# A selective scan: B's diagonals written by ScalarE, one turn of B for both directions, a shift of 64 rows, two states as products

## The chip, the cores and the metric

The kernel runs on one core of a Trainium2 chip. The time is device microseconds of one launch; the kernel before takes 25,224.66 us, the median of 3 runs (25,203.01 to 25,237.02). The profile that is quoted comes from one further execution of 25,254.47 us, with a span of 25,252.7 us from the first to the last instruction.

## What is computed

Four layers run over a batch of 8 images of 192 channels and 64 x 64 pixels in 32-bit floats. Layers 0 and 2 hold a two-dimensional selective scan, and all of the change lies there. For each image, four sequences (rows and columns, each forward and backward) of 4096 positions are scanned with 16 states a channel:

```python
x0 = x.reshape(B, D, L)
x1 = x.transpose(0, 1, 3, 2).reshape(B, D, L)
xs = jnp.stack([x0, x1, x0[..., ::-1], x1[..., ::-1]], axis=1)
x_dbl = jnp.einsum('bkdl,kcd->bkcl', xs, x_proj_weight)
dts, Bs, Cs = jnp.split(x_dbl, [R, R + N], axis=2)
dts = jnp.einsum('bkrl,kdr->bkdl', dts, dt_projs_weight)
A = -jnp.exp(A_logs.astype(jnp.float32)).reshape(K, D, N)
delta = jax.nn.softplus(dts + dt_projs_bias[None, :, :, None])

def step(h, inp):
    u_t, d_t, B_t, C_t = inp
    h = jnp.exp(d_t[..., None] * A) * h + (d_t * u_t)[..., None] * B_t[:, :, None, :]
    y = jnp.einsum('bkdn,bkn->bkd', h, C_t)
    return (h, y)
...
_, ys = jax.lax.scan(step, h0, seq)
```

So for every position, channel and state a decay `exp(dt*A)`, an input `dt*x*B`, a linear recurrence over the positions, and a sum over the 16 states weighted by C. What stands around it (norms, 1x1 and depthwise convolutions, windows and gates) is not touched.

## The kernel before

`scan_layer` is called twice for each of the 8 images, so there are 16 scans. A scan is made of **units** `(d, i, c, v)`: `d` is the direction (0 forward, 1 backward; all forward units come first), `c` one of 8 chunks of `Q = 512` positions, and `v` one of three sets of 128 rows: `v = 0` and `v = 1` are channels 0 to 127 of the one and the other orientation, `v = 2` holds channels 128 to 191 of both (`o` tells the orientations apart, 64 rows each). A scan has 2 x 8 x 3 = 48 units. Three units on one chunk, numbered `m`, are called a **group** here; a scan has 16 groups. A unit is worked in 8 **steps** `j`: each covers one of `NB = 4` blocks of `SB = 128` positions and one half (8) of the `NS = 16` states.

There is no scheduler: the loop over `k` (units) and `j` (steps) at L413 to L473 writes the instructions out by hand, and each engine executes its own in that order (`tc.manual_schedule()`). What a step issues, engine by engine:

- **VectorE**: `scan(k, j)`. For each step a small addition of the carried state to the first column (L306; every second step also a product that makes it, L304) and one hardware scan over 8 states x 128 positions (L309). The additive input is the PSUM tile `u` (two buffers), the factor and the result share the tile `da`.
- **TensorE**: `fill(k, j)` writes `u`. For 4 residues `e` and 2 ways `r` it multiplies a 32-row strip of the turned `dt*x` (`dtt`) with a 32-row strip of a matrix that has B's values on diagonals (`dg`), L288. `add_up` (L345) then sums a block's 16 states by turning each 128 x 128 piece into the PSUM tile `py`; states in `AS_PRODUCT` are multiplied by the identity, the others pass in transpose mode. `project_a/b` (L145, L152, L155) and `steps_a` (L210, L212) make B, C and dt for the group `m + 1`, `turn_a` (L226) turns `dt*x`, `diagonals_a` (L185) turns B, `turn_back` (L363) adds and turns the results of backward units.
- **ScalarE**: `decay(k + 1)` (L245, 16 exponentials of 128 x 512 for the next unit, spread over steps by `DECAY`), `cut(k + 1)` (L254, L255), which saves the first column of the next unit's decays and sets it to zero and which the next unit's first scan needs, `keep` (L316), `take` (L353, the sums out of `py`), `turn_b` (L232, L235), `project_b`'s copies (L159, L160) and `steps_b` (L216, softplus, with two loads of the activation table).
- **GpSimd**: `times_c` (L326, four a unit) and `steps_c` (L220).
- **SyncE** issues all DMAs: the loads of `vs`, C and earlier sums, the stores of C, sums and results.

What the change touches: `xd` holds the projected rows of a group (B in rows 0 to 15, C in 16 to 31, dt's inputs above, for `o = 1` the same from row 64) for 512 positions and a second copy of the first 128 behind them, so that `windows()` can take every fourth position with an offset of `r * SB + e`. The turned B comes out shifted by one block of 32 rows for `r = 1`; `turn_b` makes the matching shifted copy of `dt*x` with four copies of 32 rows (L235), and `fill` picks the strip `q = (s - r) % 4`. `diagonals_b` multiplies a mask (`msk`, 1 where column = row mod 32) with the turned B on VectorE, L195:

```python
            PUT = {(1, 7): (0, 0), (2, 0): (0, 1), (2, 2): (1, 0), (2, 3): (1, 1)}
```

says at which unit and step the four of a group are issued: after the scan of step 7 in the second unit, and of steps 0, 2 and 3 in the third. The PSUM pool `misc` has two buffers that all small TensorE products of a unit take in turn (`project`, `turn_a`, `diagonals_a`, `turn_back`, `steps_a`); a buffer comes free when ScalarE or VectorE has read it.

Of the kernel before, what the change touches and what calls it, by code (L numbers as in the profile page):

```python
# [7 lines left out]
F32 = mybir.dt.float32  # L8
AF = mybir.ActivationFunctionType
ALU = mybir.AluOpType  # L10
# [4 lines left out]
P = 128  # L15
CA, CB = 128, 64
# [4 lines left out]
Q = 512  # L21
NS = 16
SB = 128
# [17 lines left out]
def tile_net(ctx: ExitStack, tc: tile.TileContext, a: dict, out: bass.AP):  # L41
    nc = tc.nc
# [5 lines left out]
    ident = cst.tile([P, P], F32, name="ident")  # L48
# [11 lines left out]
    msk = cst.tile([P, 33], F32, name="msk")  # L60
# [38 lines left out]
    def scan_layer():  # L99
# [5 lines left out]
        with (  # L105
# [15 lines left out]
            nu, nm = len(units), len(units) // 3  # L121
            vt, xd, cdr, dg = {}, {}, {}, {}
            dts, dtx, dtt, das, cts, us = {}, {}, {}, {}, {}, {}
# [6 lines left out]
            def misc():  # L130
                return sp.tile([P, Q], F32, tag="misc", name="misc", bufs=2)
# [17 lines left out]
            def project_b(m):  # L149

                d, px = chunk_of(m)[0], pxs.pop(m)
                nc.tensor.matmul(  # L152
                    px[0:CB], wxt[:, d, 0, 0:CB], vt[m][:, 0, :], start=False, stop=True
                )
                nc.tensor.matmul(  # L155
                    px[CB:P], wxt[:, d, 0, CB:P], vt[m][:, 1, :], start=False, stop=True
                )
                xd[m] = sv.tile([P, Q + SB], F32, tag="xd", name="xd")
                nc.scalar.activation(xd[m][:, 0:Q], px, AF.Identity, bias=msk[:, 32:33])  # L159
                nc.scalar.copy(xd[m][:, Q : Q + SB], xd[m][:, 0:SB])  # L160
                cdr[m] = sd.tile([2, NB, NS, SB], F32, tag="cd", name="cd")
                for o in range(2):
                    nc.sync.dma_start(
                        out=cdr[m][o].rearrange("s n t -> n s t"),
                        in_=xd[m][o * CB + NS : o * CB + 2 * NS, 0:Q].rearrange(
                            "n (s t) -> n s t", t=SB
                        ),
                    )
# [3 lines left out]
            def windows(ways=2):  # L172
                for r in range(ways):
                    for e in range(4):
                        t0 = r * SB + e
                        yield r * 4 + e, slice(t0, t0 + 4 * P - 3, 4)

            bts = {}

            def diagonals_a(m, o):  # L180

                pt = misc()
                rows = slice(o * CB, o * CB + NS)
                for i, cols in windows():
                    nc.tensor.transpose(  # L185
                        pt[:, i * NS : (i + 1) * NS], xd[m][rows, cols], ident[rows, rows]
                    )
                bts[m, o] = pt[:, : 8 * NS].rearrange("p (i n) -> p i n", n=NS)
                dg[m, o] = sw.tile([P, 8, NS // 2, 32], F32, tag=f"dg{o}", name=f"dg{o}")

            def diagonals_b(m, o, r):

                shape = [P, 4, NS // 2, 32]
                at = slice(r * 4, (r + 1) * 4)
                nc.vector.tensor_tensor(  # L195
                    dg[m, o][:, at], msk[:, 0:32].unsqueeze(1).unsqueeze(1).to_broadcast(shape),
                    bts[m, o][:, at, r * 8 : r * 8 + 8].unsqueeze(3).to_broadcast(shape), ALU.mult,
                )


# [27 lines left out]
            def turn_b(k):  # L228

                dtt[k] = sw.tile([P, 2, 4, P], F32, tag="dtt", name="dtt")  # L230
                pt = pts.pop(k).rearrange("p (e c) -> p e c", e=4)
                nc.scalar.copy(dtt[k][:, 0], pt)  # L232
                for q in range(4):
                    r = (q + 1) % 4
                    (nc.scalar.copy if k else nc.vector.tensor_copy)(  # L235
                        dtt[k][q * 32 : (q + 1) * 32, 1], pt[r * 32 : (r + 1) * 32]
                    )

            def decay(k, n0, n1, s=slice(0, NB)):

                d, i, c, v = units[k]
                if n0 == 0 and s.start == 0:
                    das[k] = sw.tile([P, NB, NS, SB], F32, tag="da", name="da", bufs=3)
                for n in range(n0, n1):
                    nc.scalar.activation(  # L245
                        das[k][:, s, n, :], dts[k].rearrange("p (s t) -> p s t", t=SB)[:, s], AF.Exp,
                        scale=neg_a[:, v, d, n : n + 1],
                    )
# [26 lines left out]
            def fill(k, j):  # L275


                d, i, c, v = units[k]
                s = place(k, j)[0]
                u = us[k, j] = sp.tile([P, 8, SB], F32, tag="u", name="u", bufs=2)  # L280
                n = slice(j % 2 * 4, j % 2 * 4 + 4)
                for e in range(4):
                    for r in range(2):
                        q = (s - r) % 4
                        rows = slice(q * 32, (q + 1) * 32)
                        for o in ((v,) if v < 2 else (0, 1)):
                            ch = slice(0, P) if v < 2 else slice(o * CB, (o + 1) * CB)
                            nc.tensor.matmul(  # L288
                                u[ch, r * 4 : r * 4 + 4, e::4], dtt[k][rows, r, e, ch],
                                dg[k // 3, o][rows, r * 4 + e, n], start=True, stop=True,  # L290
                            )

            tmps = {}
# [79 lines left out]
                )  # L373
                nc.sync.dma_start(out=ys[v][:, c * Q : (c + 1) * Q], in_=y)

            AS_PRODUCT = (0, 5, 10)
            DECAY = (
                {0: (0, 4), 1: (4, 7), 2: (7, 11), 4: (11, 14), 5: (14, 16)},
                {0: (0, 4), 1: (4, 8), 4: (8, 12), 5: (12, 16)},
            )  # L380
            PUT = {(1, 7): (0, 0), (2, 0): (0, 1), (2, 2): (1, 0), (2, 3): (1, 1)}

            def has(k):
                return 0 <= k < nu
# [12 lines left out]
            diagonals_a(0, 0)  # L397
            steps_b(2)
            for r in range(2):
                diagonals_b(0, 0, r)  # L400
                load_c(0, r)
            turn_a(0)
            turn_b(0)
            for s in (slice(0, NB // 2), slice(NB // 2, NB)):
                decay(0, 0, NS, s)
                cut(0, s)
                if s.start == 0:
                    steps_c(1)
                    diagonals_a(0, 1)
                    fill(0, 0)  # L410
            for r in range(2):
                diagonals_b(0, 1, r)
            for k in range(nu + 1):  # L413
                m, v = divmod(k, 3)
                ahead = 0 <= m + 1 < nm
                for j in range(8):
# [27 lines left out]
                    if ahead and v == 1 and j == 1:  # L444
# [2 lines left out]
                        steps_a(k + 4)  # L447
                        steps_b(k + 3)
                        steps_b(k + 4)
                    if v > 0 and ahead and j == (6, 1)[v - 1]:  # L450
                        diagonals_a(m + 1, v - 1)
                    if (v, j) in PUT and 0 <= m + 1 < nm:
                        diagonals_b(m + 1, *PUT[v, j])
                    if j == 2:
                        if has(k - 1):
                            load_y(k - 1)
# [14 lines left out]
                            finish(k - 1)  # L471
                    if has(k + 1) and j in DECAY[v == 1]:
                        decay(k + 1, *DECAY[v == 1][j])  # L473

# [875 lines left out]
```

## Time and profile before

| what | us | instructions |
| --- | --- | --- |
| execution that was profiled | 25,254.47 | |
| its span | 25,252.7 | 511,713 |
| TensorE (PE) busy, 89% of the span | 22,469.5 | 215,432 |
| VectorE (DVE) busy, 80% | 20,274.8 | 20,869 |
| GpSimd (POOL) busy, 62% | 15,739.4 | 4,380 |
| ScalarE (ACT) busy, 58% | 14,606.7 | 23,888 |
| L309, the scans, on VectorE | 14,046.0 | 6,144 |
| L345, the sums over states, on TensorE | 8,287.3 | 58,368 |
| L288, the fills, on TensorE | 7,452.9 | 131,072 |
| L245, the decays, on ScalarE | 7,794.2 | 12,544 |
| L235, the shifted copies, on ScalarE | 1,735.5 | 3,008 |
| L195, B's diagonals, on VectorE | 1,223.5 | 1,024 |
| L185, turns of B, on TensorE | 565.7 | 4,096 |

How to read it: busy time is the time in which an engine has at least one instruction in work, over all layers. In the first scan (181.81 to 1328.92 us of the span) TensorE is busy for 1,089 of 1,147 us, VectorE for 1,039, GpSimd for 925, ScalarE for 749; between the scans the engines are much emptier. Matmuls are pipelined, so the distance from one start to the next says more of their cost than the duration of one. The page also has the TensorE clock that the throttle granted: over the first scan it is 0.93 of full speed.

A line of a timeline is: start in us, duration in us, engine, line, operation, what it writes and reads, shapes, how many in a row, and in brackets the idle time before it with what ended it. A line of a group has busy time and mean ns of one after the bar.

### The profile page before, as it was taken

What the parts mean: (1) busy time and instruction counts of PE and PEld (TensorE: products, weight loads), DVE (VectorE), ACT (ScalarE), POOL (GpSimd) and SP (SyncE); (2) the same over time, 40 slices, a digit from 0 to 9 for tenths busy, and PEclk for the clock granted to TensorE, in tenths of its full rate; (3) what the DMA queues carried; (4) which work ended last, traced back from release to release, by engine and by line L of the source; (5) the groups of instructions that cost most, each with busy time, mean ns of one, the idle gap of its engine ahead of it and who ended that gap; (6) DMA issues with size and microseconds to landing.
All of it is one profiled execution on the core that took longest, in us unless ns stands there. A gap on an engine that the chain in (4) does not pass through costs nothing.

```text
span 25252.7 us, 511713 instructions
## 1 busy us (share of the span) xinstructions
PE 22469.5 (89%) x215432; PEld 16188.8 (64%) x215432; DVE 20274.8 (80%) x20869; ACT 14606.7 (58%) x23888; POOL 15739.4 (62%) x4380
## 2 busy tenths in 40 slices
PE   9989889898898988989889898898988989889896
PEld 6847568475684756847467474674746747467473
DVE  7969779697896978969789697886978969788796
ACT  5656556564564645656456564665646656466563
POOL 5838468384783847838478384773847738477384
PEclk8989989899898998989989898898988989889898
DMA  5636556365563655636556365663655636566364
GB/s 168 208 119 209 148 172 209 119 205 148 179 208 117 207 147 176 210 118 204 144 182 207 122 207 135 185 206 119 204 137 182 207 121 206 135 185 210 119 207 121
DMA packets 1500016, 4299.01 MB, mean 170 GB/s; under 512 B 360224, under 2 KB 812672, under 8 KB 1099392
## 3 DMA queue, kind: packets, MB, share of 16 engines
q1 hardware_dynamic: 1497728, 4266.25, 56.5%
q8 instruction: 1710, 28.02, 0.5%
q14 instruction: 578, 4.73, 0.1%
HBM read 3810.55 MB, written 450.72 MB: 169 GB/s over the span
## 4 chain that ended last, share of the span: by engine, by line
PE 52%; DVE 33%; issue 5%; ACT 4%; DMA 3%; POOL 2%; SPq 1%; DVEq 0%; POOLq 0%; ACTq 0%
DVE da L309 23%; PE u L288 17%; PE py L345 16%; DVE dg L195 3%; PE pa L525 2%; PE misc L210 2%; DVE u L306 1%; PE misc L226 1%; PE pa L528 1%; PE misc L145 1%; PE misc L212 1%; PE misc L363 1%; PE misc L152 1%; ACT da L245 1%; PE paa L525 1%
## 5 line engine op out<-in xcount | busy, mean ns | idle before, releaser
L326 POOL TENSOR_TENSOR da<-da,ct 128x2048 f32<-128x2048 f32 x3056 | 13885.0, 4544 | 3580.9 <-DVE tmp L304 2297.9
L309 DVE TENSOR_TENSOR_SCAN da<-da,u 128x1024 f32<-128x1024 f32 x6144 | 14046.0, 2287 | 482.5 <-PE u L288 164.7
L345 PE MATMUL py<-ident,da 128*128 128x128 f32 x58368 | 8287.3, 292 | 0.4 <-issue 0.4
L288 PE MATMUL u<-dg,dtt 32*128 32x128 f32 x131072 | 7452.9, 291 | 873.7 <-DVE da L309 764.8
L345 PEld LDWEIGHTS py<-ident,da 128*128 128x128 f32 x58368 | 6934.3, 165 | 1412.4 <-issue 1154.0
L245 ACT ACTIVATE da<-dt,neg_a 128x512 f32<-128x512 f32 (+1 forms) x12544 | 7794.2, 700 | 21.9
L288 PEld LDWEIGHTS u<-dg,dtt 32*128 32x128 f32 x131072 | 6148.3, 168 | 2086.0 <-issue 1645.9
L220 POOL TENSOR_TENSOR dtx<-dt,vt 128x512 f32<-128x512 f32 x768 | 984.1, 1281 | 3355.3 <-ACT dt L216 3110.5
L353 ACT COPY yt<-py 128x512 f32<-128x512 f32 x768 | 450.6, 587 | 2673.7 <-PE py L345 2673.7
L306 DVE TENSOR_TENSOR u<-u,tmp 128x8 f32<-128x8 f32 x5952 | 1007.1, 169 | 1058.7 <-PE u L288 802.5
L235 ACT COPY dtt<-misc 32x512 f32<-32x512 f32 x3008 | 1735.5, 577 | 44.4
L195 DVE TENSOR_TENSOR dg<-msk,misc 128x1024 f32<-128x1024 f32 x1024 | 1223.5, 1197 | 441.0 <-PE misc L185 281.1
L316 ACT COPY carry<-da 128x16 f32<-128x16 f32 x672 | 144.4, 215 | 1678.5 <-DVE da L309 1678.4
L159 ACT ACTIVATE xd<-misc,msk 128x512 f32<-128x512 f32 x256 | 176.0, 688 | 1259.3 <-PE misc L155 1259.3
L216 ACT ACTIVATE dt<-misc 128x512 f32<-128x512 f32 x768 | 432.7, 596 | 641.4 <-PE misc L212 617.0
L969 POOL TENSOR_TENSOR acc<-u,gate 128x486 f32<-128x486 f32 (+1 forms) x80 | 108.5, 1360 | 941.5 <-DVE u L984 667.6
L925 POOL MEMSET t<- 128x4356 f32 (+2 forms) x32 | 100.5, 3141 | 933.0 <-DVE t L899 914.0
L963 PE MATMUL pwc<-t,l3taps 128*128 128x486 f32 (+1 forms) x1280 | 595.5, 614 | 40.0 <-DVE u L984 20.0
L210 PE MATMUL misc<-xd,wdt 64*128 64x512 f32 x1024 | 590.0, 680 | 13.4 <-ACT xd L159 13.4
L226 PE MATMUL misc<-ident,dtx 128*128 128x128 f32 x3072 | 590.7, 316 | 0.0
L185 PE MATMUL misc<-ident,xd 16*128 16x16 f32 x4096 | 565.7, 266 | 26.3 <-DVE dg L195 26.3
L185 PEld LDWEIGHTS misc<-ident,xd 16*128 16x128 f32 x4096 | 528.4, 210 | 94.6 <-issue 92.3
(289 smaller groups left out, 18780.7 us busy)
## 6 DMA issues: line engine op xcount, KB each, us to landing
ct<-cd SPq DMA_DIRECT2D x2048, 1024.0 KB
ct<-cd SPq DMA_DIRECT2D x2048, 512.0 KB
vt<-vs SPq DMA_DIRECT2D x768, 256.0 KB
yp<-yt SPq DMA_DIRECT2D x384, 256.0 KB
yo<-yp SPq DMA_DIRECT2D x384, 256.0 KB
ys<-y SPq DMA_DIRECT2D x384, 256.0 KB
yt<-ys SPq DMA_DIRECT2D x96, 512.0 KB
t<-ys SPq DMA_DIRECT2D x96, 512.0 KB
```

Of the source, the lines that this page charges most:

```text
L185: nc.tensor.transpose(pt[:, i * NS : (i + 1) * NS], xd[m][rows, cols], ident[rows, rows])
L195: nc.vector.tensor_tensor(dg[m, o][:, at], msk[:, 0:32].unsqueeze(1).unsqueeze(1).to_broadcast(shape), bts[m, o][:, at, r * 8 : r * 8 + 8] ...
L210: nc.tensor.matmul(pz, wdt[r, d, 0, :], x[r], start=True, stop=True)
L220: nc.gpsimd.tensor_tensor(dtx[k], dts[k], vt[k // 3][:, units[k][3], :], ALU.mult)
L226: nc.tensor.transpose(pts[k][:, i * P : (i + 1) * P], dtx[k][:, cols], ident)
L235: (nc.scalar.copy if k else nc.vector.tensor_copy)(dtt[k][q * 32 : (q + 1) * 32, 1], pt[r * 32 : (r + 1) * 32])
L245: nc.scalar.activation(das[k][:, s, n, :], dts[k].rearrange("p (s t) -> p s t", t=SB)[:, s], AF.Exp, scale=neg_a[:, v, d, n : n + 1],)
L288: nc.tensor.matmul(u[ch, r * 4 : r * 4 + 4, e::4], dtt[k][rows, r, e, ch], dg[k // 3, o][rows, r * 4 + e, n], start=True, stop=True,)
L306: nc.vector.tensor_tensor(head, head, tmps[k][:, n], ALU.add)
L309: nc.vector.tensor_tensor_scan(h, h, u.rearrange("p n t -> p (n t)")[:, way], 0.0, ALU.mult, ALU.add)
L326: nc.gpsimd.tensor_tensor(h, h, cts.pop((k, g)), ALU.mult)
L345: nc.tensor.matmul(py[k][:, s], das[k][:, s, n, :], ident, is_transpose=n not in AS_PRODUCT, start=(n == 0), stop=(n == NS - 1),)
```

## The change

The turned B is made once for both orientations: `diagonals_a(m, r)` turns all 128 rows of `xd` (four transposes of 128 x 128 for each way `r`), `diagonals_b` copies, for each way, the 8 of B's rows that it needs, of both orientations, out of PSUM into a small tile `bt`, and `diagonals_c` writes the diagonals on ScalarE, one of 32 mask columns at a time: 128 elements, each 32 elements apart in `dg`, scaled by the column of the mask. `DIAG` spreads the 32 over the steps of the three units. Only the first group of a scan still has VectorE's form (`diagonals_first`). The second way's windows are now 256 positions behind instead of 128, so `xd` carries a longer second copy (and has one buffer instead of two), the shifted copy of `dt*x` is made by two copies of 64 rows, and `fill` uses the strip `s - 2r`. `dg` is one tile for both orientations with the same total size. In `add_up` two states of 16 are products instead of three.

The diff:

```diff
--- before.py
+++ after.py
@@ -155,9 +155,9 @@
                 nc.tensor.matmul(
                     px[CB:P], wxt[:, d, 0, CB:P], vt[m][:, 1, :], start=False, stop=True
                 )
-                xd[m] = sv.tile([P, Q + SB], F32, tag="xd", name="xd")
+                xd[m] = sv.tile([P, Q + 2 * SB], F32, tag="xd", name="xd", bufs=1)
                 nc.scalar.activation(xd[m][:, 0:Q], px, AF.Identity, bias=msk[:, 32:33])
-                nc.scalar.copy(xd[m][:, Q : Q + SB], xd[m][:, 0:SB])
+                nc.scalar.copy(xd[m][:, Q : Q + 2 * SB], xd[m][:, 0 : 2 * SB])
                 cdr[m] = sd.tile([2, NB, NS, SB], F32, tag="cd", name="cd")
                 for o in range(2):
                     nc.sync.dma_start(
@@ -172,29 +172,48 @@
             def windows(ways=2):
                 for r in range(ways):
                     for e in range(4):
-                        t0 = r * SB + e
+                        t0 = 2 * r * SB + e
                         yield r * 4 + e, slice(t0, t0 + 4 * P - 3, 4)
 
-            bts = {}
-
-            def diagonals_a(m, o):
-
-                pt = misc()
-                rows = slice(o * CB, o * CB + NS)
+            bt, bps = {}, {}
+
+            def diagonals_a(m, r):
+
+                bps[m, r] = misc()
                 for i, cols in windows():
-                    nc.tensor.transpose(
-                        pt[:, i * NS : (i + 1) * NS], xd[m][rows, cols], ident[rows, rows]
+                    if i // 4 == r:
+                        nc.tensor.transpose(
+                            bps[m, r][:, i % 4 * P : (i % 4 + 1) * P], xd[m][:, cols], ident
+                        )
+
+            def diagonals_b(m, r):
+
+                if m not in bt:
+                    bt[m] = sv.tile([P, 2, 8, NS // 2], F32, tag="bt", name="bt", bufs=1)
+                rows = bps.pop((m, r)).rearrange("p (e o n) -> p o e n", e=4, o=2)
+                nc.scalar.copy(
+                    bt[m][:, :, r * 4 : r * 4 + 4], rows[:, :, :, r * 8 : r * 8 + 8]
+                )
+
+            def diagonals_c(m, i0, i1):
+
+                if m not in dg:
+                    dg[m] = sw.tile([P, 2, 8, NS // 2, 32], F32, tag="dg", name="dg")
+                for i in range(i0, i1):
+                    nc.scalar.mul(
+                        dg[m][:, :, :, :, i].rearrange("p o i n -> p (o i n)"),
+                        bt[m].rearrange("p o i n -> p (o i n)"), msk[:, i : i + 1],
                     )
-                bts[m, o] = pt[:, : 8 * NS].rearrange("p (i n) -> p i n", n=NS)
-                dg[m, o] = sw.tile([P, 8, NS // 2, 32], F32, tag=f"dg{o}", name=f"dg{o}")
-
-            def diagonals_b(m, o, r):
-
+
+            def diagonals_first(o, r):
+
+                if 0 not in dg:
+                    dg[0] = sw.tile([P, 2, 8, NS // 2, 32], F32, tag="dg", name="dg")
                 shape = [P, 4, NS // 2, 32]
                 at = slice(r * 4, (r + 1) * 4)
                 nc.vector.tensor_tensor(
-                    dg[m, o][:, at], msk[:, 0:32].unsqueeze(1).unsqueeze(1).to_broadcast(shape),
-                    bts[m, o][:, at, r * 8 : r * 8 + 8].unsqueeze(3).to_broadcast(shape), ALU.mult,
+                    dg[0][:, o, at], msk[:, 0:32].unsqueeze(1).unsqueeze(1).to_broadcast(shape),
+                    bt[0][:, o, at].unsqueeze(3).to_broadcast(shape), ALU.mult,
                 )
 
 
@@ -230,10 +249,9 @@
                 dtt[k] = sw.tile([P, 2, 4, P], F32, tag="dtt", name="dtt")
                 pt = pts.pop(k).rearrange("p (e c) -> p e c", e=4)
                 nc.scalar.copy(dtt[k][:, 0], pt)
-                for q in range(4):
-                    r = (q + 1) % 4
+                for h in range(2):
                     (nc.scalar.copy if k else nc.vector.tensor_copy)(
-                        dtt[k][q * 32 : (q + 1) * 32, 1], pt[r * 32 : (r + 1) * 32]
+                        dtt[k][h * CB : (h + 1) * CB, 1], pt[(1 - h) * CB : (2 - h) * CB]
                     )
 
             def decay(k, n0, n1, s=slice(0, NB)):
@@ -281,13 +299,13 @@
                 n = slice(j % 2 * 4, j % 2 * 4 + 4)
                 for e in range(4):
                     for r in range(2):
-                        q = (s - r) % 4
+                        q = (s - 2 * r) % 4
                         rows = slice(q * 32, (q + 1) * 32)
                         for o in ((v,) if v < 2 else (0, 1)):
                             ch = slice(0, P) if v < 2 else slice(o * CB, (o + 1) * CB)
                             nc.tensor.matmul(
                                 u[ch, r * 4 : r * 4 + 4, e::4], dtt[k][rows, r, e, ch],
-                                dg[k // 3, o][rows, r * 4 + e, n], start=True, stop=True,
+                                dg[k // 3][rows, o, r * 4 + e, n], start=True, stop=True,
                             )
 
             tmps = {}
@@ -373,12 +391,16 @@
                 )
                 nc.sync.dma_start(out=ys[v][:, c * Q : (c + 1) * Q], in_=y)
 
-            AS_PRODUCT = (0, 5, 10)
+            AS_PRODUCT = (0, 8)
             DECAY = (
                 {0: (0, 4), 1: (4, 7), 2: (7, 11), 4: (11, 14), 5: (14, 16)},
                 {0: (0, 4), 1: (4, 8), 4: (8, 12), 5: (12, 16)},
             )
-            PUT = {(1, 7): (0, 0), (2, 0): (0, 1), (2, 2): (1, 0), (2, 3): (1, 1)}
+            DIAG = (
+                {6: (0, 8), 7: (8, 13)},
+                {6: (13, 20), 7: (20, 23)},
+                {5: (23, 26), 6: (26, 32)},
+            )
 
             def has(k):
                 return 0 <= k < nu
@@ -397,7 +419,11 @@
             diagonals_a(0, 0)
             steps_b(2)
             for r in range(2):
-                diagonals_b(0, 0, r)
+                diagonals_b(0, r)
+                if r == 0:
+                    diagonals_a(0, 1)
+            for r in range(2):
+                diagonals_first(0, r)
                 load_c(0, r)
             turn_a(0)
             turn_b(0)
@@ -406,10 +432,9 @@
                 cut(0, s)
                 if s.start == 0:
                     steps_c(1)
-                    diagonals_a(0, 1)
                     fill(0, 0)
             for r in range(2):
-                diagonals_b(0, 1, r)
+                diagonals_first(1, r)
             for k in range(nu + 1):
                 m, v = divmod(k, 3)
                 ahead = 0 <= m + 1 < nm
@@ -447,10 +472,11 @@
                         steps_a(k + 4)
                         steps_b(k + 3)
                         steps_b(k + 4)
-                    if v > 0 and ahead and j == (6, 1)[v - 1]:
-                        diagonals_a(m + 1, v - 1)
-                    if (v, j) in PUT and 0 <= m + 1 < nm:
-                        diagonals_b(m + 1, *PUT[v, j])
+                    if v == 0 and ahead:
+                        if j in (3, 4):
+                            diagonals_a(m + 1, j - 3)
+                        if j in (4, 5):
+                            diagonals_b(m + 1, j - 4)
                     if j == 2:
                         if has(k - 1):
                             load_y(k - 1)
@@ -471,6 +497,8 @@
                             finish(k - 1)
                     if has(k + 1) and j in DECAY[v == 1]:
                         decay(k + 1, *DECAY[v == 1][j])
+                    if ahead and j in DIAG[v]:
+                        diagonals_c(m + 1, *DIAG[v][j])
```

## The prediction

> **What bounds the kernel now.** I read the chain of waits on the page first.
>
> ```profile
> PE 52%; DVE 33%; issue 5%; ACT 4%; DMA 3%; POOL 2%; SPq 1%; DVEq 0%; POOLq 0%; ACTq 0%
> DVE da L309 23%; PE u L288 17%; PE py L345 16%; DVE dg L195 3%; PE pa L525 2%; PE misc L210 2%; DVE u L306 1%; PE misc L226 1%; PE pa L528 1%; PE misc L145 1%; PE misc L212 1%; PE misc L363 1%; PE misc L152 1%; ACT da L245 1%; PE paa L525 1%
> ```
>
> Two engines share the chain, TensorE (PE) and VectorE (DVE); ScalarE (ACT) has 4%, and the diagonals on VectorE (L195) 3%. The starts of L309 in VectorE's timeline give the sixteen scans 18,289 us of the span of 25,252.7. A group (three units on one chunk, v = 0, 1, 2) lasts, as a mean over the scans, 81.2 us as the first of a scan, 70.4 for the other seven forward ones, 71.7 for the first seven backward ones and 67.3 as the last. All that follows is made per group; there are 7 x 16 = 112 of each middle kind.
>
> VectorE's timeline of one forward group at full clock: the units start at 1852.09, 1872.91, 1895.97, and the next group at 1919.98.
>
> ```profile
> 1875.88 0.17 DVE L306 TENSOR_TENSOR u<-u,tmp 128x8 f32<-128x8 f32 x1 [0.69 <-PE u L288]
> ...
> 1894.28 1.19 DVE L195 TENSOR_TENSOR dg<-msk,misc 128x1024 f32<-128x1024 f32 x1
> ...
> 1898.18 1.20 DVE L195 TENSOR_TENSOR dg<-msk,misc 128x1024 f32<-128x1024 f32 x1
> ```
>
> So 20.8 + 23.1 + 24.0 = 67.9 us. Eight scans with their small operations take 20.8 (4 x 2.39 + 4 x 2.81). The second unit adds 1.1 of waits for TensorE's fills and one L195, which delays the next scan by 1.11; the third adds three L195. TensorE's timeline has no gap in the first two units; in the third it waits for VectorE four times. ScalarE in the second unit and up to its next wait:
>
> ```profile
> 1885.40 0.59 ACT L353 COPY yt<-py 128x512 f32<-128x512 f32 x1 [1.63 <-PE py L345]
> 1885.88 0.59 ACT L232 COPY dtt<-misc 128x512 f32<-128x512 f32 x1
> 1886.50 2.34 ACT L235 COPY dtt<-misc 32x512 f32<-32x512 f32 x4
> 1888.87 5.01 ACT L245 ACTIVATE da<-dt,neg_a 128x512 f32<-128x512 f32 x8
> 1893.91 0.28 ACT L254 COPY da<-da 128x64 f32<-128x64 f32 x1
> ...
> 1907.02 0.59 ACT L353 COPY yt<-py 128x512 f32<-128x512 f32 x1 [5.62 <-PE py L345]
> ```
>
> The cut (L254, L255) that the next unit's first scan needs ends at 1894.54, only 1.4 us before that scan; and ScalarE stands idle in front of L353 (1.63, 5.62) where nothing behind it can use the gap. Its 58% busy is therefore no measure of its room.
>
> Third, windows of 3.41 us, the length of the shortest clock stretches, over the end of two groups (columns: PE, PEld, DVE, ACT, POOL busy, granted clock, DMA share, GB/s).
>
> ```profile
> 887.79:891.20 3.41, 2.14 (x42) 1.76 (x41) 3.27 (x5) 2.74 (x5) 0.64 (x2) 1.00 0.50 142
> 891.20:894.61 3.41, 2.77 (x32) 2.37 (x34) 3.38 (x3) 3.36 (x7) 3.41 (x1) 0.50 0.98 201
> ...
> 2109.79:2113.20 3.41, 2.13 (x45) 1.82 (x41) 3.40 (x3) 2.17 (x4) 0.81 (x1) 1.00 0.49 115
> 2113.20:2116.62 3.42, 2.11 (x41) 1.81 (x38) 3.25 (x6) 3.37 (x7) 3.25 (x1) 1.00 0.95 203
> ```
>
> After the first window the clock halves, after the other two it does not, though all are equally busy. For L345 alone the same windows have 1.10, 1.17 and 1.37 us, for L288 1.10, 1.00 and 0.81. So it is the full-height work (add-up) that counts, and the edge is near 1.1 us of it in a window. Halved stretches begin in 46 of the 112 forward groups (42 of them six windows long) and in nearly every backward one (two windows). As (70.4 - 67.9) x 112/46, a forward dip costs 6.1 us.
>
> **The change part by part.** *VectorE* loses four L195 in 15 of 16 groups: 1.1 us in the second unit, 3.2 in the third, which falls to 20.8 if nothing follows close behind.
>
> *Two products.* A product is two TensorE instructions, so a block of adding has 18 instead of 19. Ten instructions take 1.30 from start to next start (1864.43 to 1865.73), nine 1.14: about 0.11 for one, 12 blocks, -1.3 a group, of which some 0.9 lies in the two TensorE-bound units. For the clock: transposes count in these windows too, since the pair 1.10 and 1.17 holds two product passes each and differs by about one transpose. The Trainium skill, "TensorE: Matmul & The Clock Gate", Part 4, says that transposes do not count as a busy TensorE for the gate; by it this edit would put a dip into every forward group, 66 more at 6.1 us, +403 us. The two windows speak against it, and the measurement decides.
>
> *B turned for both directions.* Sixteen 16-row transposes go (eight take 1.06, 1899.44 to 1900.50), from the end of the second unit and the slack third. Eight of 128 rows come into the first unit at L226's pace (four in 0.58, 1902.96 to 1903.54): +1.2 where TensorE is the bound. And a wait comes: "misc" has two buffers, and the second four use the one that the turned dt\*x holds until L235 ends. ScalarE ends that 2.3 after it starts L353, TensorE arrives 1.1 after: 1.2 us of stall, with an add-up and the fill of step 6 queued behind. That fill now ends 0.84 before its scan.
>
> *Shift by 64.* Two copies of 64 rows for four of 32 (0.577 each): -1.17 of ScalarE a unit, between L353 and the decays. The fills read strips s and s-2 instead of s and s-1; still different strips, same instructions, so I take nothing.
>
> *Diagonals on ScalarE*, 32 multiplies of 128 elements a group with a scale pointer, each written 32 elements apart. No such row exists; the nearest:
>
> ```profile
> L245 ACT ACTIVATE da<-dt,neg_a 128x512 f32<-128x512 f32 x12032 | 7586.7, 709 | 21.8
> L245 ACT ACTIVATE da<-dt,neg_a 128x256 f32<-128x256 f32 x512 | 207.5, 492 | 0.2
> L602 ACT COPY cola<-xa 128x512 f32<-128x512 f32 x64 | 64.4, 1054 | 245.6 <-PE pb L537 245.1
> L566 ACT ACTIVATE sqb<-xnb 128x512 f32<-128x512 f32 x64 | 40.3, 630 | 16.4 <-DVE xnb L556 16.4
> L160 ACT COPY xd<-xd 128x128 f32<-128x128 f32 x256 | 76.3, 298 | 8.2
> ```
>
> L245's slope (217 ns for 256 elements) gives 0.38 for 128, and 0.08 of one overlaps the next (7586.7/12032 = 0.63 against 0.709): 0.30 each. L602, which also writes with a stride, takes 0.83 ns an element more than the dense L566: +0.11. I take 0.41, because strided it is; ends 0.30 (stride free) and 0.49 (stride, no overlap). The skill's "ScalarE: Activation LUTs", section "What ACT_TABLE_LOAD costs", has 280 ns + 0.833 an element with one pointer and 93 ns of overlap, 0.29 for 128, the same whatever the layout; by it the time would be the first rival's, and L602 disagrees.
>
> *Two small copies* of bt, about 0.3 each (L254's 0.274), and 0.1 more for the wider xd copy (L160). The single xd buffer costs nothing: its last reader, L212, is done over 40 us before the next L159, and so is the store of C. No DMA is added, moved or passed on SP's queue.
>
> **The sum for a forward group**, times from a unit's first scan. *First unit:* TensorE enters 0.7 late (below), gains 0.2 on products and has +0.6 of turns, so L353 starts at 12.4 (was 11.4). Fill to 13.5, stall to 14.7, turns 0.6, add-up 1.1, fill 1.1: step 6 scans at 17.5 (was 15.6). The rest as before less 0.2: 23.0. ScalarE: 12.4 + 2.3 + 0.3 + 1.9 + 0.3 + 1.3 + 8 x 0.41 + cut 0.6 = 22.4, in time. *Second unit:* five multiplies (2.1) and four decays (2.5) now stand before the table load and the first softplus, which ends at 6.0; the next projection needs its buffer and waits 0.5. L353 starts at 13.2 (was 12.5); + 2.3 + 5.0 + 7 x 0.41 + 0.6 = 24.0. VectorE would be ready at 22.2: **the cut is late by 1.8**. *Third unit:* L353 at 9.8, + 2.3 + 3.2 + 9 x 0.41: last column at 19.0 (the next fill waits for it, hence TensorE's 0.7), cut 19.6; VectorE's 20.8 holds. Sum 67.8, as much as now at full clock. What remains is the clock: the third unit's steps become even, 2.6 us with a full add-up in each window, so today's dips go; but 1.8 us of idle TensorE at its head can dip. I take four in ten, at 2.5 us, because four turns and the adds come two steps later and in a window like that (894.61 to 898.02) the clock came back: 68.8, that is -1.6.
>
> *Backward:* 1.0 more for turning back (L363 x8) in the first unit, 0.8 of L371 in the third, and no dip since VectorE's 0.8 shortens the idle: 23.9 + 24.0 + 21.6 = 69.5, -2.2. First groups about -2. So -(1.6 + 2.2) x 112 - 2 x 16 = -458 against the profiled 25,254.5 (span plus 1.8); that run lies 30 above the median of 25,224.7. Forecast **24,770 us**, by itself 24,500 to 25,050.
>
> **The rivals.** *ScalarE keeps up, clock full.* At 0.30 the units are 22.5, 22.7, 20.8 forward and 23.4, 22.9, 21.6 backward: 66.0 and 67.9, -4.4 and -3.8, first groups -3: 24,257. For it: ScalarE is 58% busy. Against: L602.
> *Slower: the late cut feeds the clock.* Place: head of the third unit. A window spanning a fill (1.1) and more than 1.2 us of idle has under 1.1 us of add-up; that point is passed above about 0.35 a multiply. If every forward group then dips as long as now (six windows, 6.1): 73.9, +3.5; backward unchanged: +392 - 32, 25,585. At 0.49 with short dips: units 23.6, 25.0, 21.0 and 2.4 of dips give 72.0, +1.6, and backward about 71.7: 25,380. For it: 42 of 46 forward dips are that long. Against: they began late in the third unit, past its turns.
> *No change:* the waits eat the gain exactly, 25,225.
>
> **Chances.** Forecast 0.45, first rival 0.25, slower 0.22, no change 0.08. Measurement cannot tell less than about 0.2% from nothing. Faster 0.69, same 0.08, slower 0.23. Range 24,250 to 25,450.
>
> **What would show it.** Mean of the multiplies' row (0.49 alone, 0.41 per busy time); a gap of 1.2 before the second four turns on ScalarE's L235; VectorE at the third unit's start waiting for the cut; forward halved stretches fewer than 46. I am wrong if the multiplies take 0.3, if they wait on TensorE, or if fills slow down.

## The result, and the profile after

The changed kernel takes 26,351.32 us (median of 4 runs, 26,340.78 to 26,384.32) against 25,230.84 us for the kernel before beside it (4 runs, 25,203.01 to 25,271.08): a ratio of 1.0445, 95% interval 1.0427 to 1.0463. It is 4.45% slower. The forecast was 24,770 us and the range ended at 25,450.

The profiled span is 26,339.0 us (25,252.7 before). First the page's busy times, chain and four groups (busy us, mean ns of one, idle before it and what ended that):

```profile
PE 23141.9 (88%) x210312; PEld 16527.5 (63%) x210312; DVE 19265.4 (73%) x19877; ACT 16026.7 (61%) x30576; POOL 15754.1 (60%) x4380
...
PE 57%; DVE 17%; ACT 12%; DMA 6%; issue 4%; POOL 3%; SPq 1%; DVEq 0%; POOLq 0%; ACTq 0%
PE py L363 19%; PE u L306 18%; DVE da L327 10%; ACT da L263 4%; DMA yo<-yp 4%; PE misc L229 2%; ACT dg L203 2%; PE pa L553 2%; ACT dtt L253 2%; PE misc L245 1%; PE misc L381 1%; PE misc L185 1%; PE misc L145 1%; PE misc L231 1%; PE pa L556 1%
...
L324 DVE TENSOR_TENSOR u<-u,tmp 128x8 f32<-128x8 f32 x5952 | 1008.2, 169 | 2815.6 <-PE u L306 2552.3
...
L203 ACT ACTIVATE dg<-bt,msk 128x128 f32<-128x128 f32 x7680 | 2508.2, 494 | 0.0
...
L381 PE MATMUL misc<-ident,yo 128*128 128x128 f32 x1536 | 447.1, 320 | 413.8 <-DMA yo<-yp 413.2
...
L185 PE MATMUL misc<-ident,xd 128*128 128x128 f32 x2048 | 411.4, 329 | 308.7 <-ACT dtt L253 308.1
```

Two of these groups in the kernel before (its add of the carry is L306, its turning back L363):

```profile
L306 DVE TENSOR_TENSOR u<-u,tmp 128x8 f32<-128x8 f32 x5952 | 1007.1, 169 | 1058.7 <-PE u L288 802.5
...
L363 PE MATMUL misc<-ident,yo 128*128 128x128 f32 x1536 | 407.2, 299 | 54.4 <-DMA yo<-yp 54.2
```

VectorE has left the chain as intended (33% to 17%), and now waits for TensorE's fills instead: 2,552 us ahead of L324 (803 before). New names on the chain are, among others, "ACT dg L203 2%", the new multiplies, "ACT dtt L253 2%", the copies of the turned dt\*x, and "DMA yo<-yp 4%". The last two groups say where the second and the third act: TensorE stands idle for 308 us ahead of the turns of B (L185) until ScalarE's copies are done, and for 413 us ahead of turning back (L381) until a load lands (54 us in the kernel before).

Together these waits are 0.7 ms. TensorE is also busy 672 us longer, with fewer instructions, because its clock is lower: the halved stretches in the granted clock add up to 6,892 us of the span, 4,795 before. By the starts of the scan lines the sixteen scans take 19,365 us, 1,076 more; per group:

| | forward, groups 2 to 8 | backward, groups 9 to 15 | first | last | halved clock, us |
|---|---|---|---|---|---|
| before | 70.39 | 71.70 | 81.17 | 67.27 | 4,795 |
| changed | 72.96 | 78.30 | 76.17 | 75.31 | 6,892 |

Forward, the changed groups are not alike. The ten that have the full clock throughout take 65.8 to 66.5 us, those with one halved window of 3.41 us 67.2 to 68.1, those with eight 78.3 to 79.2. In the 112 middle groups 103 halved stretches ("dips") begin, in 98 of the groups; 97 of them begin in the first unit at step 5 (52 last eight windows, 45 one). The kernel before had 46, all in the third unit. Here is TensorE's timeline of the changed kernel at that step (start, duration, what ended the idle time before):

```profile
1835.16 1.15 PE L363 MATMUL py<-ident,da 128*128 128x128 f32 x9
1836.24 1.16 PE L306 MATMUL u<-dg,dtt 32*128 32x128 f32 x16
1838.66 0.75 PE L185 MATMUL misc<-ident,xd 128*128 128x128 f32 x4 [1.26 <-ACT dtt L253]
1839.24 1.90 PE L363 MATMUL py<-ident,da 128*128 128x128 f32 x9
1841.08 1.23 PE L306 MATMUL u<-dg,dtt 32*128 32x128 f32 x8
```

Below are the windows there with the add-up alone (PE, PEld busy, granted clock, DMA share, GB/s):

```profile
1832.65:1836.06 3.41, 1.80 (x18) 1.68 (x16) 1.00 0.42 125
1836.06:1839.48 3.42, 0.49 (x6) 0.37 (x5) 1.00 0.82 307
1839.48:1842.89 3.41, 1.67 (x9) 1.26 (x7) 0.50 0.74 252
```

The second window holds a fill (1.16), the gap of 1.26, the four turns and 0.49 us of add-up; the clock halves as it ends. The turns are full-height work too, and with them the window has 1.07 us of it. The gap stands in all 224 middle groups, and at full clock in each. Counted over the trace, the clock halves after the 112 windows (97 forward, 15 backward) in which 1.06 to 1.07 us of turns and add-up stand beside it, and stays full after the 112 with 1.13 to 1.74 us.

Backward, 72 of 127 halved stretches are five windows long and begin in the third unit at step 6. TensorE and SP's queue in such a unit:

```profile
2531.87 1.25 PE L363 MATMUL py<-ident,da 128*128 128x128 f32 x9
2532.96 0.27 PE L381 MATMUL misc<-ident,yt 128*128 128x128 f32 x1
2536.82 0.47 PE L381 MATMUL misc<-ident,yo 128*128 128x128 f32 x1 [3.58 <-DMA yo<-yp]
```

```profile
2522.59 6.14 SPq L284 DMA_DIRECT2D ct<-cd  x4
2528.77 0.59 SPq L354 DMA_DIRECT2D yo<-yp  x1
```

The load of the forward result yo is issued at 2528.77, behind a load of C that waits for GpSimd to release a buffer, and is used 8.05 us later, when it has landed. TensorE wanted it after 4.5 us. The window of this gap, with the add-up alone, and the next:

```profile
2532.38:2535.80 3.42, 0.74 (x7) 0.51 (x5) 1.00 1.04 265
2535.80:2539.21 3.41, 0.00 (x0) 0.00 (x0) 0.50 0.46 188
```

Here too the clock halves as a thin window ends. The same place in the kernel before, TensorE and then SP's queue:

```profile
2545.63 0.42 PE L363 MATMUL misc<-ident,yt 128*128 128x128 f32 x1
2545.84 0.42 PE L363 MATMUL misc<-ident,yo 128*128 128x128 f32 x1
```

```profile
2537.55 0.58 SPq L336 DMA_DIRECT2D yo<-yp  x1
```

There 8.3 us lie between issue and use: the load was covered by the longer steps of the third unit. As a median over the middle backward groups, counted from the unit's first scan, the load was issued at 11.8 us and used at 20.1; in the changed kernel it is issued at 10.7 and wanted at 15.2.

### The profile page after: what moved, and what is told of

Read it like the earlier page. It is cut to its first block, busy times and chain, and to the rows that moved or that the text cites. A ratio compares the mean times of both kernels' runs of the same rounds, so it can differ in the third digit from the quotient of the medians.

```text
span 26339.0 us, 507338 instructions
## 1 busy us (share of the span) xinstructions
PE 23141.9 (88%) x210312; PEld 16527.5 (63%) x210312; DVE 19265.4 (73%) x19877; ACT 16026.7 (61%) x30576; POOL 15754.1 (60%) x4380
## 4 chain that ended last, share of the span: by engine, by line
PE 57%; DVE 17%; ACT 12%; DMA 6%; issue 4%; POOL 3%; SPq 1%; DVEq 0%; POOLq 0%; ACTq 0%
PE py L363 19%; PE u L306 18%; DVE da L327 10%; ACT da L263 4%; DMA yo<-yp 4%; PE misc L229 2%; ACT dg L203 2%; PE pa L553 2%; ACT dtt L253 2%; PE misc L245 1%; PE misc L381 1%; PE misc L185 1%; PE misc L145 1%; PE misc L231 1%; PE pa L556 1%
## 5 line engine op out<-in xcount | busy, mean ns | idle before, releaser
L306 PE MATMUL u<-dg,dtt 32*128 32x128 f32 x131072 | 7862.6, 298 | 618.8 <-DVE u L324 210.9
L363 PE MATMUL py<-ident,da 128*128 128x128 f32 x55296 | 8364.7, 302 | 6.2 <-issue 6.1
L363 PEld LDWEIGHTS py<-ident,da 128*128 128x128 f32 x55296 | 7051.5, 165 | 1569.4 <-issue 1301.9
L306 PEld LDWEIGHTS u<-dg,dtt 32*128 32x128 f32 x131072 | 6525.5, 175 | 1940.2 <-issue 1401.1
L324 DVE TENSOR_TENSOR u<-u,tmp 128x8 f32<-128x8 f32 x5952 | 1008.2, 169 | 2815.6 <-PE u L306 2552.3
L203 ACT ACTIVATE dg<-bt,msk 128x128 f32<-128x128 f32 x7680 | 2508.2, 494 | 0.0
L371 ACT COPY yt<-py 128x512 f32<-128x512 f32 x768 | 450.3, 586 | 2174.3 <-PE py L363 2174.3
L235 ACT ACTIVATE dt<-misc 128x512 f32<-128x512 f32 x768 | 431.8, 596 | 906.6 <-PE misc L231 873.8
L253 ACT COPY dtt<-misc 64x512 f32<-64x512 f32 x1504 | 872.7, 580 | 23.0
L381 PE MATMUL misc<-ident,yo 128*128 128x128 f32 x1536 | 447.1, 320 | 413.8 <-DMA yo<-yp 413.2
L229 PE MATMUL misc<-xd,wdt 64*128 64x512 f32 x1024 | 691.5, 781 | 13.4 <-ACT xd L159 13.4
L185 PE MATMUL misc<-ident,xd 128*128 128x128 f32 x2048 | 411.4, 329 | 308.7 <-ACT dtt L253 308.1
L145 PE MATMUL misc<-vt,wxt 128*128 128x512 f32 x512 | 407.5, 889 | 252.7 <-DMA vt<-vs 244.3
```

The lines of the kernel that those rows point to most:

```text
L185: nc.tensor.transpose(bps[m, r][:, i % 4 * P : (i % 4 + 1) * P], xd[m][:, cols], ident)
L203: nc.scalar.mul(dg[m][:, :, :, :, i].rearrange("p o i n -> p (o i n)"), bt[m].rearrange("p o i n -> p (o i n)"), msk[:, i : i + 1],)
L229: nc.tensor.matmul(pz, wdt[r, d, 0, :], x[r], start=True, stop=True)
L253: (nc.scalar.copy if k else nc.vector.tensor_copy)(dtt[k][h * CB : (h + 1) * CB, 1], pt[(1 - h) * CB : (2 - h) * CB])
L306: nc.tensor.matmul(u[ch, r * 4 : r * 4 + 4, e::4], dtt[k][rows, r, e, ch], dg[k // 3][rows, o, r * 4 + e, n], start=True, stop=True,)
L324: nc.vector.tensor_tensor(head, head, tmps[k][:, n], ALU.add)
```

## The experiments

Theory W says that two uncovered waits, each followed by a halved clock, cost the time; S, that ScalarE's multiplies do; P, that the dropped third product does. Ratios are to the kernel before, run beside each.

**The second four turns behind the add-up**

```
-                        if j in (3, 4):
-                            diagonals_a(m + 1, j - 3)
+                        if j == 3:
+                            diagonals_a(m + 1, 0)
...
                         add_up(block, j % 2)
+                    if v == 0 and ahead and j == 4:
+                        diagonals_a(m + 1, 1)
```

> Edit: the second four turns of B in the first unit (step 4) are issued behind that step's add-up instead of ahead of it. Theory W (two uncovered waits, each followed by a halved clock): TensorE's 1.2 us wait for ScalarE's copy of the turned dt*x is filled with the add-up, the forward dips that start at the first unit's step 5 (103 of 112 groups) mostly go, the forward group falls from 72.96 to about 67, the backward one stays at 78.3: 26,351 - 112 x 6 = about 25,680 us (25,450 to 25,950). Rival S (ScalarE's 2,508 us of multiplies is the load that sets the units): a 1.2 us wait of TensorE more or less changes nothing, within 0.5% of 26,351. Rival P (two products instead of three starve the clock gate): dips stay, only elsewhere in the group; within 0.5%.

Measured 25,199 us, ratio to the kernel before 0.9985 (0.9973 to 0.9998): 1,152 below the changed kernel, more than W's range allowed. TensorE's row for the turns:

```profile
L185 PE MATMUL misc<-ident,xd 128*128 128x128 f32 x2048 | 396.8, 320 | 17.9 <-ACT dt L235 0.9
```

The wait on ScalarE's copies is gone, and forward dips fall from 103 to 9. A forward group takes 65.5. A backward one takes 75.96, where W expected no change: it has the same gap. S and P fall for the forward groups: the same multiplies and the same two products are there.

**The load of yo first in SP's queue**

```
+                    if j == 0 and has(k - 1):
+                        load_y(k - 1)
                     if j % 2 == 0:
...
                     if j == 2:
-                        if has(k - 1):
-                            load_y(k - 1)
```

> Edit: the load of the forward result (yo) of a backward unit is issued at step 0 of the next unit, ahead of the load of C, instead of at step 2 behind it. Theory W: the 3.3 us gap of TensorE ahead of turning back in the third unit goes (414 us of idle time in front of that line become under 60), with it the five-window halved stretches that start at the third unit's step 6; the backward group falls from 78.3 to about 71, the last of a scan from 75.3 to about 68, forward unchanged at 73: 26,351 - 112 x 7.3 - 16 x 7 = about 25,420 us (25,150 to 25,750). Rival S: backward units are set by ScalarE (softplus and decays behind the multiplies); the gap moves to another line, within 0.5% of 26,351. Rival P: the same, dips begin elsewhere.

Measured 25,064 us, ratio 0.9926 (0.9901 to 0.9952), 1,287 below the changed kernel:

```profile
L381 PE MATMUL misc<-ident,yo 128*128 128x128 f32 x1536 | 358.1, 274 | 0.7 <-issue 0.7
```

The backward group falls from 78.30 to 69.07, the last from 75.31 to 63.82; forward stays at 73.01 with 100 dips. The gain was again beyond W's range.

**Both moves**

> Edit: both of the two before. Theory W: the gains add, forward about 67, backward about 71: about 24,750 us (24,450 to 25,050), under the kernel before by 1 to 3%; halved clock in all falls from 6,892 us to under 4,500. Rival S: still over 25,900. Rival P: still over 25,700.

Measured 23,943 us, ratio 0.9486 (0.9467 to 0.9505). The gains add almost exactly (1,152 + 1,287 = 2,439 against 2,408), and the time is under W's range as before. Forward 65.41, backward 67.20, 7 and 8 dips, halved clock 2,832 us. The change with both waits covered is 5.1% faster than the kernel before.

**Three products in the changed kernel** (`AS_PRODUCT = (0, 5, 10)`)

> Edit: AS_PRODUCT back to (0, 5, 10), three of sixteen passes of an add-up as products, all else as in the changed kernel. Rival P: with 19 instead of 18 instructions a block the windows hold enough, the dips of the forward groups fall to half or less (under 55 of 112) and the time to about 25,800 us or less. Theory W: a transpose counts as a product does, so both waits still halve the clock, forward dips stay over 85 of 112; TensorE has 12 x 0.11 us a group more: 26,300 to 26,650 us. Rival S: within 0.5% of 26,351.

Measured 25,690 us, ratio 1.0181 (1.0164 to 1.0198), 661 below the changed kernel, so W's expectation missed and P's time was right. But the dips do not go as P said (under 55): 71 forward ones begin, 65 of them at the same step. They are shorter: 59 of one window, 5 of seven and 1 of eight, where 52 had eight. The third product shortens most dips, and leaves their cause. Why a window more or less full decides between one and eight was not resolved.

**No product, and one, with both moves** (`AS_PRODUCT = ()`, then `(0,)`)

> Edit: on the kernel with both moves (23,943 us), AS_PRODUCT = (): all sixteen passes of an add-up are transposes, 16 instructions a block instead of 18. Theory T (a transpose keeps the clock as a product's instruction does): TensorE has 12 x 0.22 = 2.6 us a group less, the windows hold some 10% fewer full-height instructions, so a few more dips: 23,600 to 24,400 us. Theory G (only products keep the clock; the third product of the run before, 26,351 to 25,690 us, worked for that reason): with no product left in the units most of every scan runs at half clock: over 27,000 us, mean granted clock under 0.8.

> Edit: on the kernel with both moves, AS_PRODUCT = (0,), one product of sixteen passes, 17 instructions a block; between the kernels with 18 (23,943) and 16 (23,639). Theory T (a transpose keeps the clock as a product's instruction does, what is left out is only TensorE time): half-way, 23,700 to 23,880 us, mean granted clock 0.935 to 0.945. Theory G (products keep the clock): not monotone, with more halved stretches than either.

Measured 23,639 us (0.9387, 0.9363 to 0.9410) and 23,743 us (0.9410, 0.9378 to 0.9441), mean clock 0.939 and 0.941, halved clock 2,881 and 2,805 us. Theory T's times held both times. Theory G is refuted: with no product at all the add-up keeps the clock. These are the fastest versions, and beat both kernels. The granted clock over the span in 40 slices (tenths), first of the kernel with no product, then of the changed kernel:

```profile
PEclk9989999899898999989999899999999999999998
```

```profile
PEclk9889888888888888888888898898988888888887
```

The changed kernel is at 8 through most of the middle, the other at 9 for long stretches, with sixteen transposes in every add-up.

**Diagonals on VectorE again, from the turned copy in SBUF**

```
-                    if ahead and j in DIAG[v]:
-                        diagonals_c(m + 1, *DIAG[v][j])
+                    if (v, j) in PUT and ahead:
+                        diagonals_first(*PUT[v, j], m + 1)
```

> Edit: on the kernel with both moves, the diagonals are made by VectorE again, four instructions of 128x1024 at the places they had in the kernel before, out of the turned copy; ScalarE's 32 multiplies a group are left out. Theory V (VectorE's 4.8 us a group were on the path; ScalarE's multiplies lie beside other work): units as before, the second and third lengthened by 1.1 and 3.2, and dips at the third unit's long steps come back in some groups: forward 68 to 71, backward 69 to 72: 24,500 to 25,000 us. Rival S (the multiplies cost ScalarE more than VectorE gains): under 23,850 us.

Measured 26,563 us, ratio 1.0541 (1.0512 to 1.0571): both theories missed, for a reason outside them. VectorE, then GpSimd:

```profile
1907.54 1.32 DVE L214 TENSOR_TENSOR dg<-msk,bt 128x1024 f32<-128x1024 f32 x1
...
1911.56 2.78 DVE L214 TENSOR_TENSOR dg<-msk,bt 128x1024 f32<-128x1024 f32 x1
...
1919.48 3.16 DVE L214 TENSOR_TENSOR dg<-msk,bt 128x1024 f32<-128x1024 f32 x1
```

```profile
1907.95 5.30 POOL L344 TENSOR_TENSOR da<-da,ct 128x2048 f32<-128x2048 f32 x1 [0.18 <-ACT carry L334]
1917.04 4.52 POOL L344 TENSOR_TENSOR da<-da,ct 128x2048 f32<-128x2048 f32 x1 [3.79 <-DVE tmp L322]
```

An L214 that begins while GpSimd's multiply runs ends about 1.1 us after it (1919.48 + 3.16 = 1922.64, against 1917.04 + 4.52 = 1921.56): it waits for all of it. Over the trace, the 480 that began during such a multiply and ended before the next took 2,406 to 3,396 ns. Where L214 came first, GpSimd's multiply, 4.54 us as a mean in the changed kernel, took 5.30. The run says nothing of ScalarE.

**Diagonals on VectorE again, from PSUM**

```
+                    if v > 0 and ahead and j == (6, 1)[v - 1]:
+                        diagonals_a(m + 1, v - 1)
+                    if (v, j) in PUT and ahead:
+                        diagonals_v(m + 1, *PUT[v, j])
```

Here diagonals_v is VectorE's multiply of the kernel before, reading bps[m, r], the PSUM tile of the turned B. The load of yo is early, as in the run with both moves.

> Edit: on the kernel with both moves (23,943 us), the diagonals are made by VectorE at the places they had in the kernel before, and now straight out of the PSUM tile into which B was turned (four 128-row turns at the second unit's step 6, four at the third unit's step 1), so that the slow reads from SBUF of the run before (2,067 ns each as a mean, 1,318 as a median, against 1,197) are out; ScalarE's 32 multiplies and two copies a group are left out. Theory V (VectorE's 4.8 us a group were on the path, and ScalarE's multiplies lie beside other work): instructions of 1.2 us again, units as in the kernel before with the second at 23, the third at 24 to 25, halved stretches at the third unit's long steps back in 40 to 110 forward groups: 24,800 to 25,250 us. Rival S (ScalarE's part gains nothing, and the whole gain of 23,943 over the kernel before comes from the turns, the shift, the products and the early load): 23,800 to 24,150 us.

Measured 25,091 us, ratio 0.9952 (0.9937 to 0.9968):

```profile
L226 DVE TENSOR_TENSOR dg<-msk,misc 128x1024 f32<-128x1024 f32 x960 | 1147.2, 1195 | 0.0
```

Each instruction takes 1,195 ns again, and forward dips are 110. Theory V holds: moving the diagonals to ScalarE, and with them the turns of B into the first unit, is worth 25,091 - 23,943 = 1,148 us once the waits are covered; this run does not part the two. All else in the change together with the early load is worth some 140 (25,232 of the kernel before beside it, less 25,091).

**The kernel before with the early load alone, and with two products alone**

> Edit: the kernel before, with nothing but the load of the forward result issued at step 0 ahead of the load of C. Theory W: there the wait was covered (54 us of idle time ahead of turning back), so 25,230 us within 0.4%. Rival (the late load was a cost of the kernel before too): over 1% faster.

> Edit: the kernel before, with nothing but AS_PRODUCT = (0, 8) in place of (0, 5, 10). Theory T: TensorE 1.3 us a group less, but the windows near the edge hold one instruction less a block, so the halved stretches of the forward groups rise from 46 of 112 to 60 to 112: 25,000 to 25,700 us. Theory G: dips in every forward and backward group, six windows or longer: over 25,700 us. Theory N (no influence on the clock): 24,900 to 25,050 us with under 50 forward dips.

Measured 25,110 us (0.9957, 0.9944 to 0.9969) and 25,156 us (0.9978, 0.9963 to 0.9993). The load was covered there in the middle groups (backward 71.72 against 71.70); what it gains, just past W's bound, is at the scans' ends (last group 67.27 to 63.90, first 81.17 to 78.27). With two products the forward dips rise from 46 to 73, but many are short (39 of two windows), and the group falls from 70.39 to 69.64. That is what theory T said; the dropped product did not slow that kernel.

All runs, by the starts of the scans in each trace:

| | us | forward | backward | last | halved, us |
|---|---|---|---|---|---|
| turns behind the add-up | 25,199 | 65.49 | 75.96 | 76.25 | 4,851 |
| yo first | 25,064 | 73.01 | 69.07 | 63.82 | 4,897 |
| both moves | 23,943 | 65.41 | 67.20 | 63.82 | 2,832 |
| both, one product | 23,743 | 64.69 | 66.26 | 64.84 | 2,805 |
| both, no product | 23,639 | 64.33 | 65.97 | 64.45 | 2,881 |
| changed, three products | 25,690 | 68.38 | 77.17 | 72.47 | 5,204 |
| both, VectorE from SBUF | 26,563 | 76.81 | 77.57 | 65.02 | 7,031 |
| both, VectorE from PSUM | 25,091 | 70.92 | 70.14 | 63.80 | 4,495 |
| before, yo first | 25,110 | 70.49 | 71.72 | 63.90 | 4,522 |
| before, two products | 25,156 | 69.64 | 71.12 | 67.84 | 4,952 |

## Why the prediction was wrong

**The stall before the second four turns: right as a wait, unpriced as a clock event.** The prediction had it at 1.2 us at the right step, from ScalarE's L235 and the two misc buffers; it is 1.26. It entered the sum as time alone. The same text gives the condition for a dip (a window spanning a fill and more than 1.2 us of idle has under 1.1 us of add-up) but tests it only on the third unit's head. Applied to the stall, it gives what happened: a fill of 1.16 and a gap of 1.26 leave 1.0 of 3.42 us, and the window has 1.07 us of turns and add-up, under the edge of 1.1 that the prediction had read from two windows. This is the first step that failed, worth 1,152 us.

**"Backward: no dip".** The prediction gave the backward groups none because VectorE's 0.8 us of adding results (L371) shortens the idle time; the dips of the kernel before, in the third unit at its long steps, it took to go as the steps become even. Those did go. It did not ask what the long steps had been covering. In that unit the load of yo needs 8 us and had 8.3; with a shorter third unit it has 4.5. "No DMA is added, moved or passed on SP's queue" was true, and missed that its user moved. This second step is worth 1,287 us. With the load covered the third backward unit is 21.45, against the 21.6 forecast.

**The multiply: right shape, wrong overlap.** One lasts 494 ns as a mean, the upper bound (0.49). But 2,508.2 us for 7,680 is 0.327 each: 0.167 overlap the next, twice the 0.08 taken from L245. The sum used 0.41, 32 x 0.083 = 2.7 us too much in a group. So the cut was not late by 1.8: VectorE's scans wait for it 84 us in the whole program (37 before), and the second unit is 22.55 at full clock, not 24.0. The formula that the prediction quotes has no term for the layout; "the same whatever the layout" was its own reading. The main slower rival, which rested on that late cut, named the right mechanism (a dip in nearly every forward group) at the wrong place.

**What held.** Third unit 20.8: it is 20.81. First unit 23.0: 22.7 to 23.2 where the clock stays full. Products and transposes alike count for the clock: the run with no product has a mean clock of 0.939. The page "TensorE: Matmul & The Clock Gate" of the Trainium skill, Part 4, says that transposes do not count in the same way; here the measurement decides against it. The wider turns, the shift and the single xd buffer show no wait of their own in the traces beyond that for the misc buffer. One line was misread without bearing on the sum: in the third unit of the quoted group TensorE waits for VectorE six times, not four.

**The rival "ScalarE keeps up, clock full"** had 66.0 and 67.9 a group, 24,257 us. With both waits covered the kernel has 65.4 and 67.2: that rival was near the true worth of the moved work, and what it lacked was the two waits. The forecast's groups (68.8 and 69.5) were too slow for that kernel by 3.4 and 2.3 us: the run has no stall (1.2), hardly a dip (1.0 in the forecast) and multiplies that cost less than summed. With both waits gone the kernel is thus 827 us under the forecast, and below its range.

## What to carry to other kernels

Shortening a step shortens the cover of everything hidden under it: for each load used in that step, compare the time from its issue to its use before and after. Where TensorE's clock drops after a thin window, price every new wait of TensorE by the work left in its window, not by its length alone: here a wait of 1.26 us led to dips that lengthened a group by 12.7 us where they lasted eight windows (a mean of 78.8 against 66.2 at full clock).

## What was not expected of the hardware

A halved stretch outlasts its cause: after the 1.26 us gap the clock stayed halved for one window in 45 groups and for eight in 52, with TensorE busy all through the first halved windows. One more product in sixteen passes made 59 of 65 one window long. What sets the length stays open.

Little full-height work alone does not halve the clock. With no product, the trace has 982 windows at full clock in the middle groups with under 1.1 us of it but TensorE busy for 2.3 us or more, and the clock halves after one of them. In the changed kernel every window with under 1.1 us (206) was also one with TensorE busy for less than 2.3, and it halved after all. The exact condition stays open.

VectorE's 128x1024 multiply takes 1,193 to 1,198 ns when one input lies in PSUM, whether GpSimd's multiply runs or not, and 1,198 to 3,396 ns when both lie in SBUF, as it waits for a whole GpSimd instruction. The page "SBUF — State Buffer" of the Trainium skill, section "Who interferes with whom", says this of a VectorE instruction with two SBUF inputs beside a GpSimd one that reads SBUF, and that the one which starts first holds the other off; the two timelines above agree, in both orders.

ScalarE's overlap depends on the instruction: one lasts 494 ns and costs 327 ns of busy time for the 128-element multiply, 709 and 631 for the 512-element exponential (kernel before).
